# Local attention layers: outputs placed behind another tile's scores, and VectorE's products of a projected bank issued ahead of ScalarE's squares

## The chip, the core and the metric

The kernel runs on one core of a Trainium2 chip. A core has five engines that each work through their own list of instructions in order: TensorE (PE; its weight loads are told apart as PEld), VectorE (DVE), ScalarE (ACT), GpSimd (POOL) and SyncE (SP), which issues most of the DMAs. Data lies in SBUF; matmuls write to banks of PSUM. Engines wait for each other by semaphores. The metric is the time of one execution on the device in microseconds (us): the median of several runs of the same program.

## The reference

Four images of 1024 tokens and 128 features pass through two blocks with adaptive layer norms. The first block is linear attention and a routed mixture of experts. The second is a windowed attention with a global prefix, followed by a module of two local layers. Only the local layers matter here; cut to their core:

```python
def _layer(x, wqkv, qs, ksc, wo, lg, lb, w1, b1, w2, b2):
    h = shift_token(x)
    q, k, v = jnp.split(h @ wqkv, 3, axis=-1)      # 8 heads of 64
    q = l2norm(q) * qs
    k = l2norm(k) * ksc
    q, k = rotary_xpos(q, k)                        # q * cos + rotate_half(q) * sin
    o = local_attention(q, k, v)                    # windows of 64, each looks at itself and the one before
    x = x + o @ wo
    h = shift_token(x)
    h = layernorm(h) * lg + lb
    a, g = jnp.split(h @ w1 + b1, 2, axis=-1)
    return x + (a * gelu(g)) @ w2 + b2
```

All of it is in float32.

## The kernel before

The first block and the windowed attention take the first 581 us. The local layers follow: 2 layers x 4 images x 8 tiles of 128 tokens, 64 tiles in one sequence. A loop `for g in range(-1, tiles + 4)` (L1064) is a software pipeline over them. In round `g` it issues, for different tiles:

- `scores(g)` (L875): 16 matmuls in the 64x64 shape of the array (32 instructions) into two PSUM banks, then on VectorE eight masked minimum-and-add instructions (L892), one per head, which leave the scores `pr` in SBUF and their row bounds `mx`.
- `project(g + 2)` (L647): the projections to the queries (`w = 0`) and to the keys (`w = 1`) of the tile two rounds ahead, each one matmul into a bank `qk`. From a bank ScalarE takes the squares `sq` (L656) and VectorE the products with the rotary tables, `co` (L658, cosines) and `si` (L663, sines on swapped halves). VectorE sums the squares per head to `ss` (L665). Readers of one bank on different engines follow each other in the order of the program, so that `co` waits for `sq`. On POOL, `co + si` (L673) for either, and once for both `ss` is bounded (L668) and raised to the power -1/2 (L669); then the keys are scaled by it (L675). The queries' factor is given to the masked scores as a scale.
- `turn(g + 1, w)` (L838): four transposes (L845) of the queries or of the keys into a bank `qktr`; ScalarE copies the queries to `qT` (L852), VectorE the keys to `kT` (L858).
- `exps(g)` (L898): eight exponentials on ScalarE (L904), with their sums.
- `over_sums(g - 1)` (L907): VectorE's reciprocal of the sums (L912), then `pr` times it (L919): half of the heads on POOL, half on VectorE.
- `flip(g - 2, j)` (L921): transposes of `pr` (L926), copied by ScalarE to `pt` (L928).
- `outputs(g - 3)` (L931): 16 matmuls `o` of 64 columns (32 instructions, L940) from `pt` and the values `v` and `ve`, copied by ScalarE to `os` (L944). `ve` holds the values shifted by half a tile; two DMAs on SP bring it.
- `values(g - 1)` (L860), and side work by a table `steps`: `project_out` (L946) every four tiles, and the MLP in five steps (`mlp_in`, `mlp_out`, `mlp_gate`, `mlp_up`, `mlp_down`) spread over ten rounds. `mlp_gate` needs ScalarE's table of the gelu, which is loaded before it and changed back behind it.

Most of the banks of a round come from one PSUM pool, `pM`, of six buffers, so that a matmul also waits until the last reader of its bank's earlier user is done.

The order on PE is that of the program (`manual_schedule` for PE). The order on VectorE, ScalarE and POOL is made by a scheduler when the program is built, from the order of the program and its own costs; at run time it is fixed. `light` tiles (image 0 of layer 0 from tile 3) leave the sum `co + si` of the queries to PE. The first three tiles of all are projected at the end of the layer before (L821).

Of the kernel before, what the change touches and what calls it, by code (L numbers as in the profile page):

```python
# [19 lines left out]
F32 = mybir.dt.float32  # L20
BF16 = mybir.dt.bfloat16
AF = mybir.ActivationFunctionType
# [4 lines left out]
P = 128  # L27
# [9 lines left out]
HEADS, DH, DEPTH = 8, 64, 2  # L37
# [11 lines left out]
def adaln_blocks(ctx: ExitStack, tc: tile.TileContext, a: dict, out: bass.AP):  # L49
    nc = tc.nc  # L50
    pe, act, dve, pool = nc.tensor, nc.scalar, nc.vector, nc.gpsimd
# [11 lines left out]
    def bc(ap, shape):  # L63

        return ap.unsqueeze(len(ap.shape)).to_broadcast(shape)
# [579 lines left out]
    pj = ctx.enter_context(tc.tile_pool(name="pj", bufs=3))  # L645

    def project(l, b, t, w, ps):  # L647


        nt = f"{l}_{b}_{t}_{w}"  # L650
        if w == 0:
            late[l, b, t, "ss"] = pj.tile([P, 2, HEADS], F32, tag="ss", name=f"ss_{nt}", bufs=4)
        pe.matmul(ps, lhsT=hs[l, b][:, t * P : (t + 1) * P], rhs=wl[l][0][:, w, :], start=True, stop=True)  # L653
        ph = ps.rearrange("p (h e) -> p h e", e=DH)
        sq = pj.tile([P, HEADS, DH], F32, tag="sq", name=f"sq_{nt}", bufs=2)
        act.activation(sq, ph, AF.Square)  # L656
        co = pj.tile([P, HEADS, DH], F32, tag=f"co{w}", name=f"co_{nt}")
        dve.tensor_tensor(co, ph, abs_[l][:, 0, t, w, :].unsqueeze(1).to_broadcast([P, HEADS, DH]), ALU.mult)  # L658
        si = pj.tile([P, HEADS, DH], F32, tag="si", name=f"si_{nt}", bufs=3)

        ex = bass.AP(tensor=ps.tensor, offset=ps.offset + 32, ap=[ps.ap[0], [DH, HEADS], [-32, 2], [1, 32]])
        sn = abs_[l][:, 1, t, w, :].rearrange("p (i e) -> p i e", i=2).unsqueeze(1).to_broadcast([P, HEADS, 2, 32])
        dve.tensor_tensor(si.rearrange("p h (i e) -> p h i e", i=2), ex, sn, ALU.mult)  # L663
        ss = late[l, b, t, "ss"]
        dve.tensor_reduce(ss[:, w, :], sq, AX.X, ALU.add)  # L665
        if w == 1:

            pool.tensor_scalar(ss, ss, 1.0e-24, None, ALU.max)  # L668
            pool.tensor_tensor(ss, ss, nhalf[:, 0:2].unsqueeze(2).to_broadcast([P, 2, HEADS]), ALU.pow)  # L669
        if w == 0 and light(l, b, t):  # L670
            late[l, b, t, "si"] = si
        else:
            pool.tensor_tensor(co, co, si, ALU.add)  # L673
        if w == 1:
            pool.tensor_tensor(co, co, bc(ss[:, 1, :], [P, HEADS, DH]), ALU.mult)  # L675
        late[l, b, t, "co", w] = co

    def light(l, b, t):

        return (l, b) == (0, 0) and t >= EARLY  # L680
# [5 lines left out]
    with (  # L686
# [80 lines left out]
        def project_out(b, k):  # L767
            s = slice(k * BLK, (k + 1) * BLK)
            yp = ps.tile([P, BLK], F32, tag="m", name=f"y1_{b}_{k}")
            pe.matmul(yp, lhsT=wout1, rhs=kept1[b, k, "os"], start=True, stop=True)  # L770
            dve.scalar_tensor_tensor(xT[b][:, s], yp, mods[1][:, 2, b : b + 1], xT[b][:, s], ALU.mult, ALU.add)
# [18 lines left out]
        def when(g, f, *args):  # L790
            if 0 <= g < NG8:
                f(*divmod(g, NT), *args)

        for g in range(-1, NG8 + 2):
            b, t = divmod(g, NT)
            ahead = 0 <= b and b + 1 < B
            if g == -1:
                weights(0, 0)
            when(g + 2, scores)
            when(g + 2, weights)  # L800
            if ahead and t in (2, 4):
                queries(b + 1, t // 2 - 1)
            for after, k, f in ((6, 0, tokens), (8, 0, normed), (11, 1, tokens), (13, 1, normed)):
                if (g - after) % NT == 0 and 0 <= (g - after) // NT < B - 1:
                    f((g - after) // NT, k, "h3")
            for at, k, f in ((1, 0, tokens), (3, 0, normed), (5, 1, tokens), (7, 1, normed)):
                if g == at:
                    f(B - 1, k, "h2")
            when(g - 1, back)
            when(g + 1, flip, (0, 1))  # L810
            when(g + 1, values)
            when(g, outputs)
            when(g + 1, flip, (2, 3))
            if t == 5 and 0 < b <= DEPTH:
                rotary(tab, abs_[b - 1], b - 1)
            if g % 4 == 1 and g > 4:
                project_out((g - 5) // NT, (g - 5) % NT // 4)
            if ahead and t in (3, 5):
                keys(b + 1, t // 2 - 1)

            for i, w in ((0, 0), (0, 1), (1, 0), (1, 1), (2, 0), (2, 1))[max(0, g - NG8 + 6) : max(0, g - NG8 + 7)]:  # L821
                project(0, 0, i, w, ps.tile([P, BLK], F32, tag="t", name=f"qk_0_0_{i}_{w}", bufs=2))
# [6 lines left out]
    with (  # L829
# [198 lines left out]
        for l in range(DEPTH):  # L1028
            for b in range(B):
                g = (l * B + b) * NT  # L1030
# [29 lines left out]
        def project_mid(l, b, t, w):  # L1060
            if (l, b) != (0, 0) or t >= EARLY:
                project(l, b, t, w, pM.tile([P, BLK], F32, tag="mid", name=f"qk_{l}_{b}_{t}_{w}"))

        for g in range(-1, tiles + 4):  # L1064
            side = steps.get(g, [])
            when(g, scores)
            when(g + 2, project_mid, 0)

            turns = {-1: (0, 1), 0: (2,), 1: ()}.get(g, (g + 1,))
            if 1 < g < NT - 1:  # L1070
                when(g + 1, turn, 0)
            when(g - 2, flip, 0)
            when(g - 1, over_sums)
            when(g + 2, project_mid, 1)
            when(g - 2, flip, 1)
            when(g, exps)
            for i in turns:
                if not 1 < g < NT - 1:
                    when(i, turn, 0)
                if i < EARLY and g < EARLY:  # L1080
                    when(i, turn, 1)
            when(g - 3, outputs)
            if g >= EARLY - 1:
                when(g + 1, turn, 1)
            for f, args in side[:1]:
                f(*args)

            for i in {0: (), 1: (0,)}.get(g, (g - 1,)):
                when(i, values)

            f0 = g - 7
            if f0 % 4 == 0 and 0 <= f0 < tiles - NT:
                lo = f0 % NT * P
                project_out(f0 // (B * NT), f0 // NT % B, lo, lo + BLK)
            for f, args in side[1:]:
                f(*args)
# [127 lines left out]
```

## Time and profile before

| | |
|---|---|
| median of 3 runs | 1242.51 us (1238.51 to 1245.01) |
| the profiled execution | 1246.33 us, span 1244.5 us, granted clock 0.983 |
| PE busy | 1162.8 us (93%) |
| VectorE busy | 878.8 us (71%) |
| ScalarE busy | 817.8 us (66%) |
| POOL busy | 823.3 us (66%) |
| power on POOL, L669 | 64 x 2.995 us |
| products, L658 and L663 | 128 x 0.677 and 128 x 0.678 us |
| squares, L656 | 128 x 0.586 us |
| `ss`, L665 | 128 x 0.673 us |
| VectorE's `co` L658 waiting for ScalarE's `sq` L656 | 26.0 us in 23 places |

A row of the order of time gives the start, the length, the engine, the line, the operation, what it writes and reads, and how often; idle time before it and what ended it stand in brackets. A busy share near 100% says that the engine had no gap, not that its work could not be shorter. Where a row of waits names an engine, that engine's instruction came last before the wait ended.

### The profile page before, as it was taken

The page shows a single profiled execution, that of the slowest core. Times are in us where ns is not written, and L with a number is a line of the kernel's source. Part 1 is how long each engine was busy: PE and PEld are TensorE (multiplying, and loading weights), DVE is VectorE, ACT ScalarE, POOL GpSimd, SP SyncE. Part 2 cuts the span into 40 slices and gives each one's busy share as a digit, 9 for nine tenths or more (in the row PEclk, how much of TensorE's full clock was granted, in tenths as well). Part 3 has the DMA queues.
Part 4 walks back from the last instruction along what each step waited for, and adds up shares of the span by engine and source line. Part 5 has one row for each costly group of instructions (what it writes and reads, how often), then busy time and mean ns, then how long its engine had stood idle before and what let it go on. Part 6 is the DMA issues. An engine that isn't in the chain of part 4 may idle for free.

```text
span 1244.5 us, 34772 instructions
## 1 busy us (share of the span) xinstructions
PE 1162.8 (93%) x13578; PEld 714.7 (57%) x13578; DVE 878.8 (71%) x2798; ACT 817.8 (66%) x2223; POOL 823.3 (66%) x813
## 2 busy tenths in 40 slices
PE   6789999999899999988898999999999999999998
PEld 5644453534476667755665556665555556565564
DVE  5556263452476667666878988898898888998864
ACT  3363373322577677766886788788877887788862
POOL 4436445746334445444889988888899889888840
PEclk8699999999999999999999999999999999999999
DMA  6040404021400000000112111111111111111110
GB/s 179 1 130 8 138 0 132 7 74 63 137 4 4 3 20 14 11 3 3 35 27 48 27 35 26 32 40 27 39 28 34 39 29 45 38 27 31 36 40 26
DMA packets 36136, 51.04 MB, mean 41 GB/s; under 512 B 5850, under 2 KB 17668, under 8 KB 35844
## 3 DMA queue, kind: packets, MB, share of 16 engines
q1 hardware_dynamic: 35540, 48.29, 14.1%
q8 instruction: 107, 1.75, 0.6%
q10 hardware_dynamic: 432, 0.53, 0.1%
q14 instruction: 57, 0.47, 0.1%
HBM read 26.52 MB, written 2.36 MB: 23 GB/s over the span
## 4 chain that ended last, share of the span: by engine, by line
PE 43%; DVE 27%; ACT 18%; POOL 7%; issue 5%; DMA 1%; POOLq 0%; ACTq 0%; SPq 0%; DVEq 0%
ACT pr L904 5%; PE h L489 4%; PE yp L951 4%; DVE pr L892 3%; DVE co L658 3%; PE s L885 3%; DVE si L663 3%; DVE ss L665 3%; PE ptr L735 3%; PE qk L653 3%; POOL u L494 2%; ACT sq L656 2%; PE s L261 2%; PE obank L752 2%; DVE ge L997 2%
## 5 line engine op out<-in xcount | busy, mean ns | idle before, releaser
L904 ACT ACTIVATE pr<-pr,mx 128x128 f32<-128x128 f32 x512 | 200.8, 403 | 88.2 <-DVE mx L892 88.1
L673 POOL TENSOR_TENSOR co<-co,si 128x512 f32<-128x512 f32 x123 | 156.7, 1280 | 79.5 <-DVE si L663 72.2
L669 POOL TENSOR_TENSOR ss<-ss,nhalf 128x16 f32<-128x16 f32 x64 | 191.7, 2995 | 5.3
L892 DVE CUSTOM_DVE_ANT_0 pr<-s,masks,ss 128x128 f32<-128x128 f32 x512 | 144.2, 342 | 42.4 <-PE s L885 42.0
L653 PE MATMUL qk<-wqkv,hs 128*128 128x512 f32 x256 | 137.7, 620 | 4.9 <-ACT pt L737 4.9
L494 POOL TENSOR_TENSOR u<-u,cw 128x512 f32<-128x512 f32 x64 | 81.1, 1271 | 74.4 <-ACT u L492 74.4
L489 PE MATMUL h<-hT,w 128*128 128x512 f32 x256 | 123.8, 605 | 4.0 <-DVE g L496 4.0
L496 DVE TENSOR_TENSOR g<-u,h 128x512 f32<-128x512 f32 x64 | 43.8, 686 | 114.9 <-POOL u L494 114.9
L279 DVE TENSOR_REDUCE mx<-s 128x4 f32<-128x448 f32 x128 | 73.5, 617 | 56.4 <-PE s L270 56.4
L658 DVE TENSOR_TENSOR co<-qk,ab 128x512 f32<-128x512 f32 x128 | 86.7, 677 | 26.0 <-ACT sq L656 26.0
L904 ACT ACTIVATION_READ_ACCUMULATOR pr<-pr,mx 128x1 f32 x512 | 101.7, 199 | 0.0
L492 ACT ACTIVATE u<-h 128x512 f32<-128x512 f32 x64 | 38.2, 598 | 93.2 <-PE h L489 85.7
L926 PEld LDWEIGHTS ptr<-ident,pr 128*128 128x128 f32 x512 | 63.5, 141 | 61.6 <-issue 54.8
L663 DVE TENSOR_TENSOR si<-qk,ab 128x512 f32<-128x512 f32 x128 | 86.8, 678 | 0.0
L489 PEld LDWEIGHTS h<-hT,w 128*128 128x128 f32 x256 | 48.3, 194 | 66.2 <-issue 51.0
L665 DVE TENSOR_REDUCE ss<-sq 128x8 f32<-128x512 f32 x128 | 86.2, 673 | 0.0
L656 ACT ACTIVATE sq<-qk 128x512 f32<-128x512 f32 x128 | 74.9, 586 | 14.8 <-PE qk L653 12.3
L845 PE MATMUL qktr<-ident,co 128*128 128x128 f32 x492 | 76.9, 280 | 6.6 <-POOL co L675 5.3
L885 PEld LDWEIGHTS s<-kT,qT 64*64 64x64 f32 x2048 | 56.8, 134 | 45.6 <-issue 22.1
L919 POOL TENSOR_TENSOR pr<-pr,sm 128x512 f32<-128x512 f32 x64 | 74.7, 1168 | 7.9 <-DVE sm L912 7.9
L885 PE MATMUL s<-kT,qT 64*64 64x128 f32 x2048 | 72.1, 277 | 7.6 <-DVE kT L858 6.1
L737 ACT COPY pt<-ptr 112x512 f32<-112x512 f32 x128 | 72.5, 612 | 8.6 <-PE ptr L735 8.6
(212 smaller groups left out, 2871.2 us busy)
## 6 DMA issues: line engine op xcount, KB each, us to landing
cw<-cd SPq DMA_DIRECT2D x128, 128.0 KB, 3.0
ve<-vs SPq DMA_DIRECT2D x120, 128.0 KB, 2.3
hs<-hT SPq DMA_DIRECT2D x16, 256.0 KB, 3.2
out<-out SPq DMA_DIRECT2D x7, 256.0 KB, 2.7
xin<-in_x SPq DMA_DIRECT2D x3, 512.0 KB, 6.1
w<-in_w SPq DMA_DIRECT2D x3, 512.0 KB, 5.0
wqkv<-in_wqkv SPq DMA_DIRECT2D x2, 768.0 KB, 5.3
ab<-in_tab SPq DMA_DIRECT2D x1, 1024.0 KB, 7.3
```

Of the source, the lines that this page charges most:

```text
L489: pe.matmul(h, lhsT=w[:, c * P : (c + 1) * P], rhs=hT[b][:, blk(k)], start=True, stop=True)
L494: pool.tensor_tensor(u, u, kept[b, k, "cw"][:, c, :], ALU.mult)
L653: pe.matmul(ps, lhsT=hs[l, b][:, t * P : (t + 1) * P], rhs=wl[l][0][:, w, :], start=True, stop=True)
L656: act.activation(sq, ph, AF.Square)
L658: dve.tensor_tensor(co, ph, abs_[l][:, 0, t, w, :].unsqueeze(1).to_broadcast([P, HEADS, DH]), ALU.mult)
L663: dve.tensor_tensor(si.rearrange("p h (i e) -> p h i e", i=2), ex, sn, ALU.mult)
L665: dve.tensor_reduce(ss[:, w, :], sq, AX.X, ALU.add)
L669: pool.tensor_tensor(ss, ss, nhalf[:, 0:2].unsqueeze(2).to_broadcast([P, 2, HEADS]), ALU.pow)
L673: pool.tensor_tensor(co, co, si, ALU.add)
L885: pe.matmul(S[j][qs, c, :], lhsT=q[rw, c, qs], rhs=k[rw, c, at : at + P], start=True, stop=True)
L892: dve.tensor_tensor_reduce(out=pr[:, c, :], in0=S[j][:, c, :], in1=mk[:, min(t, 1), :], scale=kept[l, b, t, "ss"][:, 0, h : h + 1], scalar ...
L904: act.activation(pr[:, c, :], pr[:, c, :], AF.Exp, bias=mx[:, j, c : c + 1], scale=-1.0, accum_out=sm[:, j, c : c + 1])
```

## The change

Two edits. In `project` the squares (`sq`, ScalarE) are issued behind the two products (`co` and `si`, VectorE) of the same bank instead of ahead of them; the sum `ss` stays where it was, behind `sq`. Since readers of one bank follow each other, `co` no longer waits for `sq`, and `sq` waits for `si`. In the loop `outputs(g - 3)` moves from between the turns of the queries and of the keys up to directly behind `scores(g)`, ahead of the projection of the queries. No instruction is added, removed or resized. The line numbers move: after the change `co` is L656, `si` L661 and `sq` L663.

```diff
@@ project
-        sq = pj.tile([P, HEADS, DH], F32, tag="sq", name=f"sq_{nt}", bufs=2)
-        act.activation(sq, ph, AF.Square)
         co = pj.tile([P, HEADS, DH], F32, tag=f"co{w}", name=f"co_{nt}")
         dve.tensor_tensor(co, ph, abs_[l][:, 0, t, w, :].unsqueeze(1).to_broadcast([P, HEADS, DH]), ALU.mult)
...
         dve.tensor_tensor(si.rearrange("p h (i e) -> p h i e", i=2), ex, sn, ALU.mult)
+        sq = pj.tile([P, HEADS, DH], F32, tag="sq", name=f"sq_{nt}", bufs=2)
+        act.activation(sq, ph, AF.Square)
         ss = late[l, b, t, "ss"]
         dve.tensor_reduce(ss[:, w, :], sq, AX.X, ALU.add)
@@ the loop over rounds
             when(g, scores)
+            when(g - 3, outputs)
             when(g + 2, project_mid, 0)
...
                 if i < EARLY and g < EARLY:
                     when(i, turn, 1)
-            when(g - 3, outputs)
             if g >= EARLY - 1:
                 when(g + 1, turn, 1)
```

## The prediction

> **What bounds the kernel now.** I read the busy table by stretches first, then the chain that ended last, the waits, and last the order of time of one cycle. The local layers (64 tiles of 128 tokens, from 581 us to about 1204 us) repeat a cycle of four tiles, told apart by their side work: A (gate of the MLP, ScalarE's table changed to gelu and back), B (up, and the statistics of the next part), C (down), D (output projection). One cycle, tile by tile:
>
> ```profile
> 963.98:973.35 9.37, 9.37 (x94) 5.64 (x93) 7.96 (x26) 7.68 (x24) 7.87 (x8) 1.00 0.07 18
> 973.35:983.42 10.07, 10.02 (x102) 5.85 (x101) 8.03 (x26) 9.62 (x28) 7.84 (x7) 1.00 0.28 67
> 983.42:993.09 9.67, 9.44 (x97) 5.74 (x93) 9.67 (x41) 6.56 (x24) 8.99 (x8) 1.00 0.12 27
> 993.09:1003.75 10.66, 10.66 (x99) 6.53 (x99) 8.60 (x28) 7.61 (x25) 10.33 (x9) 1.00 0.16 38
> ```
>
> Columns after the length: busy us of PE, weight loads, DVE, ACT, POOL, then clock and DMA. PE has no slack in any tile, so at first sight the order on PE is worth something. But ACT fills B (9.62 of 10.07), DVE fills C (9.67 of 9.67), POOL nearly fills D (10.33 of 10.66): each neighbour takes over for one tile. So I priced the hand-over from C to D. POOL, in order of time:
>
> ```profile
> 990.57 1.48 POOL L919 TENSOR_TENSOR pr<-pr,sm 128x512 f32<-128x512 f32 x1
> 992.01 1.26 POOL L673 TENSOR_TENSOR co<-co,si 128x512 f32<-128x512 f32 x1
> 993.36 0.26 POOL L668 TENSOR_SCALAR ss<-ss 128x16 f32<-128x16 f32 x1
> 993.70 2.92 POOL L669 TENSOR_TENSOR ss<-ss,nhalf 128x16 f32<-128x16 f32 x1
> 996.71 1.04 POOL L675 TENSOR_TENSOR co<-co,ss 128x512 f32<-128x512 f32 x1
> 997.71 1.04 POOL L919 TENSOR_TENSOR pr<-pr,sm 128x512 f32<-128x512 f32 x1
> ```
>
> The scaled keys (L675) end at 997.75. PE turns them in D:
>
> ```profile
> 997.35 0.34 PE L940 MATMUL o<-pt,ve 128*64 128x64 f32 x4
> 998.43 0.66 PE L845 MATMUL qktr<-ident,co 128*128 128x128 f32 x4
> 998.92 0.60 PE L160 MATMUL out_m<-ident,xh_m 128*128 128x128 f32 x4
> ```
>
> So the second turn, at 998.43, has 0.68 us to spare; after it PE needs 5.32 us to the next tile (1003.75). VectorE in C and at the start of D, which feeds POOL:
>
> ```profile
> 987.97 0.68 DVE L658 TENSOR_TENSOR co<-qk,ab 128x512 f32<-128x512 f32 x1
> 988.58 0.68 DVE L663 TENSOR_TENSOR si<-qk,ab 128x512 f32<-128x512 f32 x1
> 989.17 0.67 DVE L665 TENSOR_REDUCE ss<-sq 128x8 f32<-128x512 f32 x1
> ...
> 991.67 0.67 DVE L665 TENSOR_REDUCE ss<-sq 128x8 f32<-128x512 f32 x1
> 992.27 0.67 DVE L858 COPY kT<-qktr 128x512 f32<-128x512 f32 x1
> 992.87 0.73 DVE L1004 SCALAR_TENSOR_TENSOR hT<-ym,cols,hT 128x512 f32<-128x512 f32 x1
> 993.52 0.19 DVE L912 RECIPROCAL sm<-sm 128x8 f32<-128x8 f32 x1
> 993.75 0.72 DVE L919 TENSOR_TENSOR pr<-pr,sm 128x512 f32<-128x512 f32 x1
> ```
>
> **Outputs behind the scores.** No instruction is added. In the PE rows of tile A four transposes take 0.43 us between neighbours of their own shape (967.28 to 967.71). Before outputs they take 0.53 (967.71 to 968.24); the first outputs row lasts 0.17 against 0.12, the last 0.22, the transposes behind them 0.49: 0.31 us for entering and leaving the 64-column shape. The scores pay 0.09 on entry (0.52 from the last yp against 0.43), 0.16 inside (1.04 against eight groups of 0.11), and 0.10 on the projection behind them (0.96 against 0.86). That is 0.66 per tile. With scores and outputs adjacent, one exit and one entry go. The passage from 64x64 to 128x64 is in no row: at most it costs what the scores' exit and the outputs' entry do together (saving 0.16 a tile), at least nothing (0.32). I take 0.16, since both shapes reload weights: at most 64 x 0.16 = 10 us, if PE ends every wait.
>
> The Trainium skill, "TensorEngine Tiling (Array Packing)", Key Properties, says that a change of tiling mode drains TensorE. Both shapes are modes of their own there, so three drains would stand for four, a quarter of the 0.66, about 10 us over all tiles (an estimate); the trace's rows give the same. It speaks for the change.
>
> The projections move 1.1 us later behind the scores. Hidden: their first result is there 3.4 us after the scores' start, and VectorE is busy with the masked scores until 3.44 in A (967.42) and 4.55 in C; were that cover gone, each late 0.1 us would push VectorE by 0.1. The outputs run 3.2 us earlier; their copies `ve` were issued a whole tile before (about 10 us, against 2.3 us to landing), and SP's order is unchanged. ScalarE's copy `os` now stands between the exponentials, 2.4 us after the scores' start, with the outputs done at 2.2.
>
> **Products ahead of the squares.** The wait of `co` for `sq` goes (26.0 us in the list of waits, 0.78 of it in B). In its place `sq` waits for `si`, and `ss` still for `sq`. The order of the built program on each engine tells what is queued behind. In B, ScalarE runs exp, os, pt, two exps, pt, sq, two exps, sq: at the spacings of the rows (exp 0.39, the others 0.47) from 976.64 the second square ends at 981.03. VectorE's second reduction follows it, and L997 starts at 981.66 instead of 981.83: 0.17 us gained.
>
> In C the order is worse. ScalarE: exp, os, two exps, pt, two exps, pt, two exps, and only then sq. From 985.52 (the second exp waits for its masked scores, 986.08 + 0.39) the first square stands at 989.75 to 990.32, against 985.92 before. VectorE: co, si, reciprocal, co reach 989.87 and wait there 0.48 us for the square. Then, 0.60 to 0.65 apart as in the rows above, ss at 990.35, L919 990.95, si 991.59, kT 992.19, L1004 992.79, the second ss 993.44 to 994.11, reciprocal to 994.23. Before, the second ss ended at 992.34: 1.77 us later, 0.65 of that because L1004 now stands ahead of it. kT ends at 992.86, before the scores' start of 993.09, so the scores of D are not late.
>
> POOL: L668 follows at 994.19. In seven cycles (counted from 0: those whose C projects tile 4 of image 2, 0 and 4 of image 3 in layer 0, and 0 and 4 of images 0 and 1 in layer 1) the built program now puts L919 between L668 and the power L669, where it stood behind L675. It waits for the reciprocal (994.23) and starts at 994.5. Its price is 1.04 (as at 997.71) or 1.48 (as at 990.57, where VectorE's own L919 had started 0.14 us before). VectorE's L919 starts at the same reciprocal here, so I take 1.48. Then L669 996.0, L675 999.0 to 1000.05, and the turn at 1000.1 instead of 998.43: 1.67 later, less the 0.17 from B, 1.5 us per cycle (1.05 with the short row). Seven cycles: 10.5 us (7.4).
>
> The Trainium skill, "SBUF — State Buffer", two separate sides, says that VectorE with two SBUF inputs and GpSimd hold one port pair as an exclusive lock for a whole instruction. It speaks against the change here: full blocking behind a 0.72 instruction begun 0.14 earlier would make 1.62 of 1.04 (an estimate), where the trace shows 1.48.
>
> In the other six cycles L669 follows L668 at once (994.53): L675 ends at 998.55, the turn comes at 998.6 less 0.17, as before: 0. There too the turn waits for POOL, so PE's 0.16 a tile is not collected; bounds -0.6 (four tiles of 0.16) and +0.5 each.
>
> **The light tiles** (four, 600 to 635 us, 8.57 apart). Now ScalarE's second square ends the chain: exp, sq, exps, qT, pt, exps, sq, co, si, ss, kT. Afterwards: first exp at 1.66, eight exps and os 3.55, sq 0.57, hence ss at 5.8, then co, si, kT (0.6 each, 0.67): 8.25 and 0.04 to the scores, 0.28 gained, -1.1 us in all; bounds 0 (L675 late by the L919 ahead of it) and -1.5.
>
> From 635 to 690 us POOL is nearly without a gap, its work only reordered: I take 0; L919 ahead of the power can hold two turns by 1.0 each, +2, and co free of sq can give 1 back. The last tiles and the three projected in the layer before: 0 to -1, taken as 0.
>
> **Sum.** +10.5 - 1.1 = +9.4 us. The profiled execution took 1246.33 (span 1244.5), 0.3% over the median of 1242.51; it would take 1255.7, the median 1252.
>
> **Rivals.** (1) *The PE order pays*: if L675 in D is no later than the turn, PE's saving counts. For: PE is busy in 39.49 of the cycle's 39.77 us. Against: 1.77 us of delay meet 0.68 of slack. Price: 13 cycles of 0.6, 7.8, with the light tiles 9: 1234. It decides if the second ss in C ends before about 992.9. (2) *A wash*: the stall comes without the port's lock and with the passage free elsewhere: 7 x 1.05 = 7.4, less 6 x 0.6 and 1.1: 1245. (3) *The change does not do what it says*: one ScalarE-VectorE wait merely replaces the other and POOL's order is covered: 1242. (4) *The early stretch is hit as well* (+2), and the six cycles by 0.5: 1257.
>
> **How the numbers follow.** Forecast (1248 to 1256) 0.50, rival 4 0.10, rival 2 0.14, rival 3 0.10, rival 1 0.16. A measurement tells 0.5% (6.2 us) from no change. Slower takes the forecast, rival 4 and a little of rival 2: 0.62; rivals 2 and 3 make most of same, 0.22; rival 1 faster, 0.16. The range 1236 to 1260 leaves most of rival 1 out below and the sum of all upper bounds above; the forecast's own range is 1248 to 1256.
>
> **What would show it.** Right: L845 waiting for POOL L675 about 1.5 us once per cycle in seven cycles, cycles of 41.2 us there and 39.8 in the others; POOL L919 of 1.48 between L668 and L669; VectorE's ss waiting for sq in C; light tiles 8.3 apart; scores and outputs adjacent saving 0.16. Wrong: cycles under 39.5, or L675 ending ahead of the turn.

## The result, and the profile after

The changed kernel took 1261.28 us in the median of five executions (1259.07 to 1265.24), the kernel of before 1242.13 beside it (1238.51 to 1245.01): 1.0158 times as long, 95% interval 1.0132 to 1.0184. The forecast was 1252, its range ended at 1260. The profiled execution took 1265.24 us (span 1263.4), 18.9 more than that of before. The scores' starts on PE say where (us, between the starts of the tiles named):

| stretch | before | after | forecast of the difference | difference |
|---|---|---|---|---|
| tiles 0 to 8 (the light ones in it) | 64.27 | 64.44 | -1.1 | +0.2 |
| tiles 8 to 20 | 119.40 | 123.75 | +1.5 | +4.4 |
| tiles 20 to 44 (six cycles) | 238.80 | 249.99 | +9.0 | +11.2 |
| tiles 44 to 60 (four cycles) | 161.44 | 165.16 | 0 | +3.7 |
| tile 60 to the end | 79.35 | 78.62 | 0 | -0.7 |

(The seventh cycle with L919 ahead of the power, the one that starts with tile 16, lies in the second row.) In the first two rows the granted clock differs too: in the execution of before tiles 2 and 3 ran at 0.92 and 0.91, in that of after tiles 10 and 11 at 0.97 and 0.77; from tile 12 to 62 it is 1.00 in both. One cycle of after by tiles A, B, C, D, from the view by stretches; its columns are those shown for before:

```profile
977.98:987.20 9.22, 9.22 (x94) 5.66 (x93) 8.11 (x26) 7.53 (x24) 7.06 (x7) 1.00 0.01 2
987.20:996.90 9.70, 9.70 (x102) 6.07 (x101) 7.70 (x25) 9.67 (x28) 7.85 (x7) 1.00 0.29 69
996.90:1007.43 10.53, 9.29 (x95) 5.75 (x93) 10.10 (x41) 6.57 (x24) 8.45 (x8) 1.00 0.12 27
1007.43:1019.65 12.22, 10.73 (x99) 6.53 (x99) 9.40 (x29) 7.65 (x25) 11.62 (x10) 1.00 0.19 44
```

A and B got shorter by 0.15 and 0.37, C longer by 0.86, D by 1.56. PE is busy for 9.29 of the 10.53 us of C and now has gaps in both C and D. VectorE in C, in order of time, with what ended the idle time before an instruction in brackets:

```profile
1003.16 0.64 DVE L656 TENSOR_TENSOR co<-qk,ab 128x512 f32<-128x512 f32 x1
1004.23 0.69 DVE L665 TENSOR_REDUCE ss<-sq 128x8 f32<-128x512 f32 x1 [0.43 <-ACT sq L663]
1004.83 1.26 DVE L919 TENSOR_TENSOR pr<-pr,sm 128x512 f32<-128x512 f32 x1
1006.01 0.68 DVE L661 TENSOR_TENSOR si<-qk,ab 128x512 f32<-128x512 f32 x1
1006.61 0.67 DVE L858 COPY kT<-qktr 128x512 f32<-128x512 f32 x1
1007.21 0.73 DVE L1004 SCALAR_TENSOR_TENSOR hT<-ym,cols,hT 128x512 f32<-128x512 f32 x1
1007.87 0.67 DVE L665 TENSOR_REDUCE ss<-sq 128x8 f32<-128x512 f32 x1
```

The first reduction waits for the square, as forecast (0.43 us; 0.48 was worked out), and L1004 stands ahead of the second one. But L919 takes 1.26 us where 0.64 to 0.72 was put, and `kT` ends at 1007.28. POOL over the same time and into D:

```profile
1004.50 1.04 POOL L919 TENSOR_TENSOR pr<-pr,sm 128x512 f32<-128x512 f32 x1
1006.83 1.28 POOL L673 TENSOR_TENSOR co<-co,si 128x512 f32<-128x512 f32 x1 [1.29 <-DVE si L661]
1008.63 0.26 POOL L668 TENSOR_SCALAR ss<-ss 128x16 f32<-128x16 f32 x1 [0.52 <-DVE ss L665]
1008.85 1.42 POOL L919 TENSOR_TENSOR pr<-pr,sm 128x512 f32<-128x512 f32 x1
1010.23 2.92 POOL L669 TENSOR_TENSOR ss<-ss,nhalf 128x16 f32<-128x16 f32 x1
1013.23 1.04 POOL L675 TENSOR_TENSOR co<-co,ss 128x512 f32<-128x512 f32 x1
```

And PE, which pays twice:

```profile
1007.43 1.10 PE L885 MATMUL s<-kT,qT 64*64 64x128 f32 x32 [1.25 <-ACT sq L663]
...
1014.33 0.66 PE L845 MATMUL qktr<-ident,co 128*128 128x128 f32 x4 [1.48 <-POOL co L675]
```

The second wait is the forecast one. The first, 1.25 us before the scores of D, was forecast not to be. The row names the second square, but the scores take their banks from a PSUM pool of their own (`pS` in the kernel), which no square reads. They start 0.15 us after the end of `kT` (1007.28), just as in before, where the squares were early, `kT` ended at 992.94, and PE waited already:

```profile
993.09 1.10 PE L885 MATMUL s<-kT,qT 64*64 64x128 f32 x32 [0.23 <-DVE kT L858]
```

So in both kernels it is `kT` that the scores of D wait for.

### The profile page after: what moved, and what is told of

The parts are those of the page before. It is cut to its first block, busy times and chain, and to the rows that moved or that the text cites. A ratio compares the mean times of both kernels' runs of the same rounds, so it can differ in the third digit from the quotient of the medians.

```text
span 1263.4 us, 34806 instructions
## 1 busy us (share of the span) xinstructions
PE 1157.9 (92%) x13578; PEld 720.2 (57%) x13578; DVE 898.0 (71%) x2798; ACT 819.1 (65%) x2223; POOL 820.1 (65%) x813
## 4 chain that ended last, share of the span: by engine, by line
ACT 20%; DVE 15%; PE 14%; POOL 6%; issue 2%; DMA 0%; ACTq 0%; POOLq 0%; DVEq 0%
ACT pr L904 8%; PE yp L951 4%; DVE ss L665 3%; POOL ss L669 3%; ACT sq L663 3%; DVE pr L892 2%; PE s L885 2%; DVE ge L997 2%; ACT pt L928 2%; ACT ge L990 2%; DVE si L661 1%; DVE pr L919 1%; ACT os L944 1%; DVE kT L858 1%; ACT L904 1%
## 5 line engine op out<-in xcount | busy, mean ns | idle before, releaser
L673 POOL TENSOR_TENSOR co<-co,si 128x512 f32<-128x512 f32 x123 | 155.8, 1281 | 73.1 <-DVE si L661 67.6
L669 POOL TENSOR_TENSOR ss<-ss,nhalf 128x16 f32<-128x16 f32 x64 | 187.4, 2929 | 2.9
L904 ACT ACTIVATION_READ_ACCUMULATOR pr<-pr,mx 128x1 f32 x512 | 98.4, 192 | 0.0
L663 ACT ACTIVATE sq<-qk 128x512 f32<-128x512 f32 x128 | 75.5, 590 | 33.5 <-DVE si L661 31.0
L656 DVE TENSOR_TENSOR co<-qk,ab 128x512 f32<-128x512 f32 x128 | 86.7, 677 | 10.6 <-PE qk L653 10.6
L661 DVE TENSOR_TENSOR si<-qk,ab 128x512 f32<-128x512 f32 x128 | 86.8, 678 | 0.0
L845 PE MATMUL qktr<-ident,co 128*128 128x128 f32 x492 | 67.5, 275 | 20.8 <-POOL co L675 19.8
L919 POOL TENSOR_TENSOR pr<-pr,sm 128x512 f32<-128x512 f32 x64 | 80.0, 1251 | 8.1 <-DVE sm L912 8.1
```

What stands on the lines that cost most here:

```text
L904: act.activation(pr[:, c, :], pr[:, c, :], AF.Exp, bias=mx[:, j, c : c + 1], scale=-1.0, accum_out=sm[:, j, c : c + 1])
L919: eng.tensor_tensor(pr, pr, bc(sm[:, j, :], [P, 4, P]), ALU.mult)
```

## The experiments

Each kernel was timed beside the kernel of before, and the ratios are to that. This table has them all, with the lengths of the four tiles in the cycle that starts with tile 24 (from the starts of the scores):

| kernel | median us | ratio (95%) | A | B | C | D | cycle |
|---|---|---|---|---|---|---|---|
| before | 1242.1 to 1244.8 | 1 | 9.37 | 10.07 | 9.67 | 10.66 | 39.77 |
| after | 1261.28 | 1.0158 (1.0132 to 1.0184) | 9.21 | 9.70 | 10.54 | 12.21 | 41.66 |
| products alone | 1253.21 | 1.0074 (1.0048 to 1.0099) | 9.36 | 9.95 | 9.48 | 12.30 | 41.09 |
| outputs alone | 1255.61 | 1.0091 (1.0068 to 1.0114) | 9.22 | 9.98 | 10.50 | 10.51 | 40.21 |
| L919 pinned | 1250.64 | 1.0049 (1.0031 to 1.0067) | 9.22 | 9.70 | 10.53 | 11.22 | 40.67 |
| reduction first | 1247.96 | 1.0017 (1.0000 to 1.0035) | 9.21 | 9.71 | 10.54 | 11.02 | 40.48 |
| C alone | 1256.79 | 1.0110 (1.0077 to 1.0143) | 9.37 | 10.06 | 9.57 | 12.30 | 41.30 |
| C undone | 1241.96 | 0.9981 (0.9965 to 0.9998) | 9.21 | 9.70 | 10.14 | 10.51 | 39.56 |
| C undone, L919 pinned | 1242.47 | 0.9985 (0.9963 to 1.0008) | 9.21 | 9.69 | 10.15 | 10.51 | 39.56 |
| products in B only | 1241.83 | 0.9992 (0.9973 to 1.0011) | 9.22 | 9.74 | 10.14 | 10.51 | 39.61 |
| B's sums apart | 1234.75 | 0.9934 (0.9912 to 0.9956) | 9.21 | 9.70 | 9.42 | 11.21 | 39.55 |
| squares back in A and D | 1231.88 | 0.9894 (0.9872 to 0.9916) | 9.22 | 9.76 | 9.42 | 10.52 | 38.92 |

The theory was the late chain of the prediction: C's late square, the second reduction behind L1004, L919 ahead of the power. The main rival: the new order on PE itself costs the time.

**Each edit alone.** The second edit without the first leaves the outputs where they were:

```diff
-            when(g - 3, outputs)
             when(g + 2, project_mid, 0)
...
+            when(g - 3, outputs)
             if g >= EARLY - 1:
```

> Only the second edit (products ahead of the squares); the outputs stay at the tile's end. Theory (late chain): the loss sits in C and D, where the first square follows the exponentials on ScalarE, the second reduction follows L1004 on VectorE and L919 stands ahead of the power on POOL, so that PE waits for L675 at L845 in D. In the built order the square of C stands even behind the queries' copy, so the cycle should be about 41.7 us as in the changed kernel, plus what that one saved on PE in A and B (0.15 each): 41.7 to 42.0 against 39.77 before, 13 cycles of 1.9 to 2.2: 1264 to 1270 us. Rival (PE order: outputs behind the scores is what costs): without that edit the time falls back to 1240 to 1247.

1253.21 us: outside both forecasts. D is about as long as in the changed kernel (12.30), which is the theory's part, but C is 9.48: in this order VectorE does L919 (1.31 us) while the square is made, so that it needs 4.96 us from `co` of C to the end of `kT`, as much as before (4.97), and the loss is 1.3 us a cycle instead of 1.9. L919 is long here although it starts 0.73 us ahead of POOL's half, for POOL's sum L673 is running at that time (VectorE's row, then POOL's):

```profile
996.09 1.31 DVE L919 TENSOR_TENSOR pr<-pr,sm 128x512 f32<-128x512 f32 x1
...
995.59 1.27 POOL L673 TENSOR_TENSOR co<-co,si 128x512 f32<-128x512 f32 x1 [0.39 <-DVE si L661]
996.82 1.49 POOL L919 TENSOR_TENSOR pr<-pr,sm 128x512 f32<-128x512 f32 x1
```

The first edit without the second keeps the squares first:

```diff
+        sq = pj.tile([P, HEADS, DH], F32, tag="sq", name=f"sq_{nt}", bufs=2)
+        act.activation(sq, ph, AF.Square)
         co = pj.tile([P, HEADS, DH], F32, tag=f"co{w}", name=f"co_{nt}")
...
-        sq = pj.tile([P, HEADS, DH], F32, tag="sq", name=f"sq_{nt}", bufs=2)
-        act.activation(sq, ph, AF.Square)
```

> Only the first edit (outputs behind the scores); the squares stay ahead of the products. Theory (late chain): the keys' chain of C keeps its order of before (second reduction ahead of L1004, power ahead of L919), so L675 is in time and PE collects its saving, 0.15 us a tile and 0.6 a cycle: 13 cycles 7.8 us, less up to 0.5 a cycle in A or D where VectorE waits for a square that now comes behind ScalarE's copy of the outputs: 1234 to 1241 us. Rival (PE order costs): the loss stays, 1254 to 1262. Second rival (the first projection, 1.1 us later behind scores and outputs, pushes VectorE in each tile and eats the saving): 1242 to 1248.

1255.61 us. The number falls in the first rival's range and refutes the theory's claim that this edit gains by itself; the tiles tell that PE's order is not what costs. A and D are 0.15 shorter, as PE's saving has it. C is 0.83 longer, and its chain begins in B (chain of waits, start, length, what):

```profile
984.73 0.47 ACT os L944
985.20 0.51 ACT sq L656
985.70 0.02 issue
985.73 0.69 DVE co L658
```

ScalarE's copy `os` of the outputs now stands ahead of B's first square. In before, `co` of B started 4.30 us after the scores' start (977.65 against 973.35), here 4.98 (985.73 against 980.75), and VectorE has work without a gap from there to C's `kT`. The light tiles lose more: 7.1 us of the 9.2 by which the profiled executions differ lie between tiles 3 and 7. In the one that starts at 621.55 the second square, which the tile's last products wait for, begins 6.65 us after the scores' start; in the one of before at 618.18 it was 5.42. One of these tiles also ran at a granted clock of 0.85, so that 1.6 of the 7.1 us go with the clock. The first edit needs the second: only with the products ahead of the square does `co` not wait for it in B. The 9 and 12 us of the two edits are different losses, the one in D, the other in C and the light tiles; that they add up to about the whole is a coincidence.

**L919 pinned.** In the changed kernel POOL's half of L919 goes behind L675 again:

```diff
-            pool.tensor_tensor(co, co, bc(ss[:, 1, :], [P, HEADS, DH]), ALU.mult)
+            late["scaled"] = pool.tensor_tensor(co, co, bc(ss[:, 1, :], [P, HEADS, DH]), ALU.mult)
...
-                        eng.tensor_tensor(pr, pr, bc(sm[:, j, :], [P, 4, P]), ALU.mult)
+                        with ExitStack() as behind:
+                            if eng is pool:
+                                behind.enter_context(tc.issue_after(kept["scaled"].ins))
+                            eng.tensor_tensor(pr, pr, bc(sm[:, j, :], [P, 4, P]), ALU.mult)
```

> The changed kernel with one order pinned: POOL's half of L919 goes behind L675 again, so that the power L669 follows L668 at once. Theory (late chain): the seven cycles of 41.66 us lose the 1.42 us that L919 took there, down to where the other six stand (40.8): 7 x 0.85 = 6 us, and 0 to 4 us more between 645 and 770 us, where L919 also stood ahead of the power: 1251 to 1256 us, still slower than before by the late second reduction. Rival (L919 delayed merely holds the next transposes of the probabilities): 1258 to 1263.

1250.64 us, 10.6 less, just below the forecast. The power now follows L668 at once, and D is 1.0 us shorter. POOL in this kernel, in order of time:

```profile
954.34 0.26 POOL L668 TENSOR_SCALAR ss<-ss 128x16 f32<-128x16 f32 x1 [0.52 <-DVE ss L665]
954.68 3.19 POOL L669 TENSOR_TENSOR ss<-ss,nhalf 128x16 f32<-128x16 f32 x1
957.94 1.04 POOL L675 TENSOR_TENSOR co<-co,ss 128x512 f32<-128x512 f32 x1
```

The power itself took 3.19 instead of 2.92; VectorE's half of L919, begun at 954.39, still ran when it started. The stretch of tiles 8 to 20 came back whole (119.38 against 123.75). L919 ahead of the power is not shown to be all of that loss: 1.5 us of it lie in tile 11, which took 13.35 us at a granted clock of 0.77 in the changed kernel and 11.85 at 1.00 here. The four cycles from tile 44, where C's keys never had that order, did not move (165.17).

**The reduction first.** On top of that, L1004 behind the second reduction:

```diff
-        dve.tensor_reduce(ss[:, w, :], sq, AX.X, ALU.add)
+        late["reduced"] = dve.tensor_reduce(ss[:, w, :], sq, AX.X, ALU.add)
...
-            dve.scalar_tensor_tensor(yT[b][:, s], y, cols[:, V_B2 + l : V_B2 + l + 1], yT[b][:, s], ALU.add, ALU.add)
+            with tc.issue_after(kept["reduced"].ins):
+                dve.scalar_tensor_tensor(yT[b][:, s], y, cols[:, V_B2 + l : V_B2 + l + 1], yT[b][:, s], ALU.add, ALU.add)
```

> The run with POOL's L919 pinned, and L1004 behind the second reduction in C. Theory: L1004 ahead of that reduction is 0.66 us of the late chain; with it behind (a reciprocal of 0.11 comes ahead instead) the turn in D comes 0.55 us earlier: cycles of 40.1 instead of 40.67 us, 13 x 0.55 = 7 us: 1242 to 1246 us. Rival (the second square on ScalarE, behind the queries' copy, is as late as the reduction): 1248 to 1251.

1247.96 us, a gain of 2.7 by the medians (4 by the ratios) instead of 7. The number stands just below the rival's range, but not for the rival's reason: the turn no longer waits. D stays at 11.02, since something else is late next, which neither forecast had named. PE in D, in order of time:

```profile
955.40 1.04 PE L845 MATMUL qktr<-ident,co 128*128 128x128 f32 x8
...
957.12 1.13 PE L864 MATMUL v<-wqkv,hs 128*128 128x512 f32 x2 [0.24 <-ACT sq L663]
```

The values' matmul waits for D's own first square, which the second edit puts behind seven exponentials (it ends at 957.07).

**C alone, and C undone.** The edit is made by the tile's place; tiles 0 and 4 of each image are projected in C. In the changed kernel, with C undone:

```diff
+        sq = pj.tile([P, HEADS, DH], F32, tag="sq", name=f"sq_{nt}", bufs=2)
+        first = t % 4 == 0
+        if first:
+            act.activation(sq, ph, AF.Square)
         co = pj.tile([P, HEADS, DH], F32, tag=f"co{w}", name=f"co_{nt}")
...
-        sq = pj.tile([P, HEADS, DH], F32, tag="sq", name=f"sq_{nt}", bufs=2)
-        act.activation(sq, ph, AF.Square)
+        if not first:
+            act.activation(sq, ph, AF.Square)
```

> The changed kernel with the second edit undone in tile C alone (the banks of tiles 0 and 4 of each image have their square ahead of the products again). Theory (late chain): C's second reduction is early again and POOL runs the power at once, so PE in D waits no longer and both savings are collected: 0.15 us a tile on PE and 0.17 in B, cycles of 39.0 to 39.3, 13 x 0.5 to 0.75 = 6 to 10 us under before, the light tiles 1 more, the stretch from 645 to 770 us 0 to 4 us worse than before: 1231 to 1239 us. Rival (PE order, or the products in all four tiles): no more than a quarter to a half of the loss goes, 1250 to 1257.

1241.96 us: the 19 us are gone with this one tile's order. D takes 10.51 and its second turn waits for nothing. The gain below before that the theory wanted is mostly missing. A part is lost in tile 6, in whose round the second image's tile 0 is projected: 9.95 us instead of 8.58. The larger part is C, which takes 10.14: ScalarE works without a gap from A's exponentials to B's square, then VectorE without a gap to C's `kT`, and PE waits for that. First VectorE in C, then PE at the start of D, in order of time:

```profile
982.65 0.64 DVE L660 TENSOR_TENSOR co<-qk,ab 128x512 f32<-128x512 f32 x1
983.21 0.79 DVE L923 TENSOR_TENSOR pr<-pr,sm 128x512 f32<-128x512 f32 x1
983.91 0.68 DVE L665 TENSOR_TENSOR si<-qk,ab 128x512 f32<-128x512 f32 x1
984.52 0.67 DVE L669 TENSOR_REDUCE ss<-sq 128x8 f32<-128x512 f32 x1
985.11 0.67 DVE L862 COPY kT<-qktr 128x512 f32<-128x512 f32 x1
...
985.93 1.10 PE L889 MATMUL s<-kT,qT 64*64 64x128 f32 x32 [0.84 <-DVE kT L862]
```

The counterpart has the kernel of before with the products ahead in C alone (`first = t % 4 != 0`, outputs at the tile's end):

> The kernel of before with the products ahead of the squares in tile C alone (the banks of tiles 0 and 4 of each image); outputs at the tile's end. Theory (late chain: it takes only C's late square, the second reduction behind L1004 and L919 ahead of the power): the loss of the second edit alone (9 us) comes back whole and its small gain in B is missing: cycles of 41.2 to 41.4 us, 1253 to 1258 us. Rival (the products cost a little in every tile): a quarter of it, 1245 to 1247.

1256.79 us, as forecast: 1.1% slower by a quarter of the second edit. Per cycle this is 1.5 us, where the whole edit, with its gain in B, cost 1.3. With C undone, the pin adds nothing:

> C undone as in the run before, and POOL's half of L919 behind L675 in every tile. Theory: with C undone the keys are in time, so POOL's order binds no cycle any more: cycles stay at 39.5 to 39.6 us; 0 to 2 us are gained in the light tiles and up to 770 us: 1239 to 1243 us. Rival (POOL's order still holds the turn): another 4 to 8 us gained, 1234 to 1238.

1242.47 us, as expected, and it says less than it seems to: with C undone L919 already stands behind L675 again for C's keys, and the pin moves it only in the other tiles (D's and A's power had it ahead), where it costs nothing: cycles of 39.56 in both. With the products ahead in B and the light tiles alone (`first = not (t % 4 == 3 or light(l, b, t))`):

> The changed kernel with the products ahead of the squares in B and the light tiles alone, squares ahead in A, C and D. Theory (outputs behind the scores cost 11.6 us by themselves because ScalarE's copy of the outputs makes B's first square 0.5 to 0.7 us late, VectorE waits for it, and each light tile gets 1.5 us longer): the products are needed in B and the light tiles only: cycles of 39.5 to 39.7 us, 1239 to 1245 us. Rival (A and D need them too): 1247 to 1254.

1241.83 us, cycles of 39.61: A and D do not need the second edit.

**A version that beats both.** C's chain has VectorE's half of L919 and its reciprocal in it, for the sums of B, though their transposes come only in D. They are taken apart, on top of C undone and L919 pinned:

```diff
-        def over_sums(l, b, t):
+        def over_sums(l, b, t, js=(0, 1)):
...
-                dve.reciprocal(sm, sm)
+                if 0 in js:
+                    dve.reciprocal(sm, sm)
...
+                    if j not in js:
+                        continue
...
+        def apart(g):
+            return g % 4 == 1 and g > NT
...
-            when(g - 1, over_sums)
+            if not apart(g - 1):
+                when(g - 1, over_sums)
...
                 when(g + 1, turn, 1)
+            if apart(g - 1):
+                when(g - 1, over_sums, (1,))
+            if apart(g):
+                when(g, over_sums, (0,))
```

> As the run with C undone and POOL's L919 behind L675, and besides the probabilities of B normalised apart: reciprocal and POOL's half in B, VectorE's half behind the keys' copy of C instead of ahead of it. Theory (with C undone the bound is a chain of ScalarE in A and B and VectorE from B's square to C's keys' copy, at whose end PE waits 0.84 us): 0.82 us of that chain goes, and POOL's half leaves C, so that L675 comes earlier too: C 9.45 instead of 10.14 us, cycles of 38.9 us, 13 x 0.65 = 8 us under the run with both edits: 1230 to 1236 us. VectorE's L919 costs 0.60 to 0.72 there, with no L919 of POOL beside it. Rival (POOL's L675, only 0.16 us ahead of the turn in D there, takes over): 1238 to 1242.

1234.75 us, inside the theory's range, but not for its reason alone: C came to 9.42 as worked out, and D gave all of it back (11.21), again by the values' matmul behind D's square (PE in D, in order of time):

```profile
954.92 1.12 PE L868 MATMUL v<-wqkv,hs 128*128 128x512 f32 x2 [0.44 <-ACT sq L667]
```

Over the run without this edit the profiled execution gained 2.9 us from tile 44 to 60 and 0.6 before tile 20, less than the 7.7 between the medians. The blocks ahead of the local layers, which no run edits, alone take 574.9 to 583.7 us in the profiled executions; how much of the rest is this spread stays open. Since A and D do not need the products ahead, their squares go back (`first = t % 4 == 0 or t % 4 != 3 and not light(l, b, t)`):

> The run with B's probabilities normalised apart, and the squares ahead of the products again in A and D too; the products stay ahead in B and in the light tiles but tile 4. Theory: in the run with B apart D took 11.21 us because the values' matmul at L868 waits for a square that stands behind seven exponentials on ScalarE (0.70 us a cycle, just what C had gained); with the square back behind three exponentials D takes 10.51 and C keeps 9.42: cycles of 38.85 to 38.95 us, 11 cycles x 0.65 = 7 us under that run: 1225 to 1231 us. Rival (D waits for something else, such as POOL's L675 or VectorE's masked scores, 0.7 us later behind L923's half): 1232 to 1238.

1231.88 us, 0.9 above the expected range, with the cycles as expected (38.92), and 1.1% under before. One cycle by stretches:

```profile
911.43:920.65 9.22, 9.22 (x94) 5.66 (x93) 8.01 (x26) 7.53 (x24) 7.70 (x6) 1.00 0.13 31
920.65:930.42 9.77, 9.77 (x102) 6.12 (x102) 7.70 (x26) 9.74 (x28) 8.37 (x7) 1.00 0.12 29
930.42:939.84 9.42, 9.29 (x94) 5.75 (x93) 9.42 (x40) 6.50 (x24) 9.02 (x8) 1.00 0.12 29
939.84:950.35 10.51, 10.51 (x99) 6.54 (x99) 9.34 (x29) 7.70 (x25) 9.70 (x10) 1.00 0.12 27
```

PE is busy for 38.79 of 38.92 us.

## Why the prediction was wrong

**Right.** The sign, and the place and order of the mechanism. C's square stands behind the exponentials, VectorE waits for it, L1004 and then POOL's L919 come ahead of the power, and the second turn in D waits: 1.55 us more in D, where the working has 1.67, or 1.5 with B's gain. Undoing C alone takes the whole loss away, and C alone makes 13 of the 19 us. The terms as measured: the square's wait 0.43 (0.48), POOL's L919 1.42 (1.48), the scores and outputs side by side 0.15 a tile in A (0.16). That last size is partly luck, since the bounds around it do not hold: the passage from scores to outputs costs only about 0.04 (in A the first outputs row lasts 0.16 against 0.12), and what is saved is the 0.10 of the transposes ahead of the outputs and the 0.06 of those behind.

**The step that failed** is the sentence "kT ends at 992.86, before the scores' start of 993.09, so the scores of D are not late". The 993.09 was no fixed start: in before PE waited 0.22 to 0.30 us there for `kT` in every cycle from tile 16 on, so that each delay of `kT` passes on in full. In after the scores of D come 0.79 to 0.88 us later in the tile, in every cycle from tile 20 on. Two things make up the 0.86 of the cycle shown. VectorE's L919 was carried along at its old 0.64; it takes 1.18 on the chain, because the wait for the square put it 0.33 us behind POOL's L919 instead of 0.14 ahead of it. With this C needs 5.43 us from `co` to the end of `kT`, where the prediction's times give 4.89 and before took 4.97: +0.46 against before. The rest, 0.40, is that C now begins earlier against VectorE: its first `co` comes 4.95 us after the scores' start instead of 4.55. A and B together got shorter by 0.52, but counted from A's start that `co` came only 0.12 earlier (23.87 instead of 23.99), since the chain through ScalarE and VectorE did not follow. The forecast counted what was at stake at D's turn alone; the delay has two exits from C, `kT` to the scores and `ss` to POOL, and both were open. Per cycle: -0.15 -0.37 +0.86 +1.55 = +1.89 against +1.5.

**The six other cycles** were put at 0 and the four that repeat cleanly (from tile 44) cost 0.9 each: 0.5 less in A and B, the same 0.8 more in C, and 0.6 more in D. There the second reduction ends 1.11 us after the scores' start, where in before it ended 0.74 ahead of it, and the turn waits 0.65 us for the keys. On POOL two changes nearly cancel: L668 took 0.69 instead of 0.26, beside VectorE's L1006, and the power 2.92 instead of 3.47, which in before was the one beside L1006. The pin left these cycles alone, C undone took most of it off (162.07 against 165.16).

**The stretch from tile 8 to 20** beyond its one counted cycle was taken as 0 with +2 as a bound; it was +2.9. The bound's cause, L919 ahead of the power, has a part in it, as the pinned run shows; up to 1.5 of it goes with the low clock of tile 11 (0.77), and how much belongs to each stays open.

**The light tiles** were to be 8.3 us apart and to gain 1.1. The three of 8.57 became 8.45, 8.45 and 8.58, pinned or not: 0.2 in all. L919, named in the bound, cost 0.7 in tile 3 (9.41, pinned 8.73) and 0.9 in tile 7 (10.96, pinned 10.07), all four at a clock of 1.00. Pinned, the whole stretch takes 62.88, 1.4 less than before, but this is near the 1.1 by luck: 1.1 of it lies in tiles 2 and 3, which ran at 0.92 and 0.91 in before and at 1.00 there.

**B** gained 0.37, not 0.17: the products alone bring 0.12 there, and the outputs' move 0.25 on top. So PE's saving was collected, as in A, although the prediction had said that it "is not collected".

**The rivals.** Rival 1, that PE's order pays, assumed that the outputs move without a cost on ScalarE. The run of outputs alone shows the cost: `os` ahead of B's square. "Hidden" was argued for the projections from VectorE's side only; ScalarE's copy was named, and not priced. Rival 4 had the right places and was put at 1257 with a chance of 0.10. What was not priced at all: in D the values' matmul starts only when D's late first square has ended (L864, L868), and with that square ahead of the products again D fell from 11.21 to 10.52. In the changed kernel the turn's wait covers it. Of the 9.5 us by which the sum of 9.4 was short, 6.6 lie in the two stretches taken as 0 (2.9 and 3.7), 2.2 in the six counted cycles and 1.3 in tiles 0 to 8; 0.5 came back at the two ends.

The Trainium skill, "SBUF — State Buffer", two separate sides, states that the shared port pair goes to whichever of the two engines starts first, for the whole instruction. Here that rule shows in both directions, in rows of this case. In before VectorE's L919 started 0.14 us ahead and POOL's took 1.48; in after POOL's started 0.33 ahead, took 1.04, and VectorE's took 1.26. A full block gives an end at 1004.50 + 1.04 + 0.72 = 1006.26 (an estimate); the row ends at 1006.09. For the power the rule does not show: while it runs, VectorE's L919 takes 0.68 to 0.72 (last section). The prediction had used the rule for POOL's second L919 and not asked who is first at the other pair.

The 0.40 us in C come with the outputs' move, as the run with products alone tells: there the first `co` comes 4.45 us after the scores' start, even earlier than before, and 23.77 after A's. The move adds 0.50 to that: A and B shorter by 0.40, `co` later by 0.10.

Open: no run did nothing but keep the two halves of L919 apart. That VectorE's is held up by POOL is read from the rows of all kernels (last section); in the run with B's sums apart, where POOL's half stands in another tile, it takes 0.77 on the chain. The 2.9 us between tiles 8 and 20 were not divided between the order and the clock.

## What to carry to other kernels

Where several engines take turns as the bound, an edit that frees one must be priced in each tile by its own order: here one reordering was needed in B, of no use in A and D, and cost 13 to 19 us in C. A start that is itself set by a wait is not slack: look in the profile for what released it before counting on it. A late instruction has several exits (here `kT` to the scores, `ss` to POOL, the square to the values' matmul); follow each one to PE, because behind the wait that is removed the next one stood only a few tenths of a us away. When two engines' instructions change places in time by a few tenths, ask which of them now comes first, and what the other one's engine is running at that moment, not only its counterpart.

## What the runs showed of the hardware

VectorE and POOL hold each other up by fixed amounts. In the twelve profiled executions, from tile 18 to 62, VectorE's L919 (128x512) that begins while POOL has 0.14 us or more left of a multiply or sum of 128x512 ends 0.54 to 0.56 us after that instruction of POOL, in all 216 cases. So its length is set by what is left: 0.72 with 0.17 left (before, 990.43), 1.26 with 0.71 left (after, 1004.83), 1.31 with 0.76 left (products alone, 996.09). While POOL's power runs it is not held up: 0.68 to 0.72.

The other way, POOL's L919 that begins behind VectorE's ends 0.90 us after it, in all 161 cases, and takes 1.23 to 1.51 instead of 1.04. Small operations of POOL stretch too. Begun beside VectorE's L919, L668 (128x16) takes 0.58 to 0.76 instead of 0.26 and ends 0.11 after it; the power takes 3.19 to 3.34 instead of 2.92 and ends 2.78 after it.

In the run with outputs alone one light tile, before which PE had stood idle for 1.90 us, had a granted clock of 0.85 and took 11.49 us, where the next two, at 1.00, took 9.89 and 9.90; whether the idle time is the reason was not tried. Its length alone does not decide: before the second turn of tile 2 PE stands idle for 2.57 us in the run with products alone, where that tile has a clock of 0.87, and in the changed kernel, where it has 1.00.
